# Layer 0 of a four-layer graph network: the key and query products of four blocks by Strassen's seven half-size products

## The chip, the core and the metric

The kernel runs as one program on one core of a Trainium2 chip. The metric is the device time of one execution in microseconds (us), as the median of several runs; lower is better. Everything is computed in fp32.

## What is computed

The network has four layers over a graph of N = 2708 nodes with 512 features each. Each layer adds the result of its graph operation to its input and normalises the rows. The change touches the first step of layer 0, a multi-head attention with 8 heads of 64 dimensions, masked by the adjacency matrix:

```python
keys    = jnp.einsum('nj,hjk->hnk', node_matrix, Wks)
queries = jnp.einsum('nj,hjk->hnk', node_matrix, Wqs)
values  = jnp.einsum('nj,hjk->hnk', node_matrix, Wvs)
atts = jnp.einsum('hqk,hmk->hqm', queries, keys) / key_dim ** 0.5
atts = atts - 1e+16 * (1.0 - adj)[None, :, :]
atts = jax.nn.softmax(atts, axis=-1)
return jnp.einsum('hqm,hmk,hko->qo', atts, values, Wo)
```

Taken over all heads, keys, queries and values are each one product of the 2708x512 node matrix with a 512x512 weight matrix.

## The kernel before

**Projections.** The nodes are split into NB = 6 blocks of 512 columns of the transposed node matrix; the last, block 5, has only 148. A block is loaded into the tile `xb` (128 partitions, KC = 4 slices of the 512 features, up to 512 nodes; two buffers). For each block in turn, 0 to 5, the loop at L215 does three projections. Keys: for each of the NP = 4 groups of 128 output features, `project_in` (L227 to L237) accumulates four matmuls of 128x128 weights with 512 moving columns in one PSUM bank, and the result is copied into `KT` by `evac`, which sends copies to VectorE (L85) and ScalarE (L87) in turn. Block 0 has its four groups interleaved (L243), so that the first slices can be used as they land. Values: GpSimd first makes `xp`, a copy of the block with its columns in another order (L264, one buffer), and for each 128 nodes four matmuls (L269) with 512 moving columns go into `V`. Queries: `project_in` again, with ScalarE scaling by 1/8 on the way out into `qb` (L280, two buffers), and GpSimd's queue stores `qb` to DRAM tiles `qtd`, 128 nodes at a time (L283). The pool `ps_0` gives these products four of the eight PSUM banks.

After block 3 has been written down (L284), the code loads the adjacency rows of the first 128 nodes, sums and masks them, and loads their queries back from `qtd` as `qt` (L177).

After the loop, eight slices of a weight matrix `gw` that layer 2 needs are loaded, multiplied by a vector `ga` and reduced to `u` (L294 to L299). They depend on nothing in layer 0, so that this work runs early, next to block 0.

**Attention.** Then come 84 pairs of a group of 128 query nodes and a pair of heads, and one last item for the remaining 20 nodes. The order on TensorE, VectorE and ScalarE is written out by hand here. `pss` (L329) are the scores, for which VectorE adds the mask and takes maxima (L351, into `s`), ScalarE takes exponentials (L373), VectorE transposes (L380) into `d`, DMAs deal out `d` to `e` (L390), and `av` (L436) sums the values. The scores of the first pair need `qt` of the first chunk and all of `KT`. They use four PSUM banks of the pool `ps_s`; before, these are the four that `ps_0` has not used.

**What sets the order in the projections.** A scheduler orders each engine's instructions by when it expects their inputs. Each engine then works through its own list without overtaking, and waits are semaphores. TensorE's list follows the program: K, V, Q of block 0, of block 1, and so on, then the first scores.

**Layer 3** already uses seven products of halves for a multiplication with the adjacency matrix (L1160), with 512 moving columns, and with 256 in its last group of nodes.

Of the kernel before, what the change touches and what calls it, by code (L numbers as in the profile page):

```python
# [8 lines left out]
F32 = mybir.dt.float32  # L9
AF = mybir.ActivationFunctionType  # L10
ALU = mybir.AluOpType
AX = mybir.AxisListType
PSUM = bass.MemoryType.PSUM
DRAM = bass.MemoryType.DRAM

P = 128
BLK = 512
# [5 lines left out]
def kernel(  # L23
# [22 lines left out]
    nc = tc.nc  # L46
    N, D = x.shape
    KD = 64
    NP = wq.shape[1] // P
    KC = D // P  # L50
    NC = (N + P - 1) // P
    NB = (N + BLK - 1) // BLK
    QSCALE = 1.0 / KD**0.5

    def rows(c):
        return c * P, min(P, N - c * P)

    def cols(b):
        return b * BLK, min(BLK, N - b * BLK)

    def chunks_of(b):
        n0, w = cols(b)
        return [n0 // P + i for i in range((w + P - 1) // P)]
# [18 lines left out]
    def evac(dst, src, every=2):  # L82
        turn[0] += 1
        if turn[0] % every == 0:
            nc.vector.tensor_copy(dst, src)  # L85
        else:
            nc.scalar.copy(dst, src)  # L87
# [24 lines left out]
    def load_rows(t, src):  # L112
        nc.sync.dma_start(t, src.rearrange("(k p) f -> p k f", p=P))
# [24 lines left out]
    with ExitStack() as l0:  # L138
# [3 lines left out]
        KT = kvp.tile([P, NP, N], F32, tag="KT", name="KT")  # L142
        V = kvp.tile([P, NC, D], F32, tag="V", name="V")
# [4 lines left out]
        qtd = [dram.tile([P, NP, rows(c)[1]], F32, tag=f"qtd{c}", name=f"qtd{c}") for c in range(NC)]  # L148
# [58 lines left out]
            nc.scalar.activation(a, a, AF.Identity, scale=1e16, bias=far)  # L207

        with tc.tile_pool(name="kvw", bufs=1) as kvw, tc.tile_pool(name="xTb", bufs=2) as xtp, tc.tile_pool(
            name="ps_0", bufs=4, space=PSUM  # L210
        ) as ps_0:
            wk_sb = kvw.tile([P, KC, D], F32, tag="wk", name="wk_sb")
            wv_sb = kvw.tile([P, KC, D], F32, tag="wv", name="wv_sb")
            wq_sb = kvw.tile([P, KC, D], F32, tag="wq", name="wq_sb")
            for b in range(NB):  # L215
                n0, w = cols(b)
                xb = xtp.tile([P, KC, BLK], F32, tag="xb", name=f"xb{b}")
                if b == 0:
                    for k in range(KC):
                        nc.sync.dma_start(wk_sb[:, k, :], wk[k * P : (k + 1) * P, :])  # L220
                        nc.sync.dma_start(xb[:, k, :w], xT[k * P : (k + 1) * P, n0 : n0 + w])
                    load_rows(wv_sb, wv)
                    load_rows(wq_sb, wq)
                else:
                    load_rows(xb[:, :, :w], xT[:, n0 : n0 + w])

                def project_in(w_sb, p, name):  # L227
                    ps = ps_0.tile([P, BLK], F32, tag="t", name=name)
                    for k in range(KC):
                        nc.tensor.matmul(  # L230
                            ps[:, :w],
                            w_sb[:, k, p * P : (p + 1) * P],
                            xb[:, k, :w],
                            start=(k == 0),
                            stop=(k == KC - 1),
                        )
                    return ps  # L237

                if b == 0:
                    pk = [ps_0.tile([P, BLK], F32, tag="t", name=f"psk0_{p}") for p in range(NP)]  # L240
                    for k in range(KC):
                        for p in range(NP):
                            nc.tensor.matmul(  # L243
                                pk[p][:, :w],
                                wk_sb[:, k, p * P : (p + 1) * P],
                                xb[:, k, :w],
                                start=(k == 0),
                                stop=(k == KC - 1),
                            )
                else:  # L250
                    pk = (project_in(wk_sb, p, f"psk{b}_{p}") for p in range(NP))
                for p, ps in enumerate(pk):
                    evac(KT[:, p, n0 : n0 + w], ps[:, :w])


                xp = xtp.tile([P, KC, BLK], F32, tag="xp", name=f"xp{b}", bufs=1)
                for c in chunks_of(b):
                    o, q = rows(c)[0] - n0, rows(c)[1]
                    src = xb[:, :, o : o + q]
                    dst = xp[:, :, o : o + q]  # L260
                    if c < ND:
                        src = src.rearrange("p k (i x) -> p k x i", i=KD4)
                        dst = dst.rearrange("p k (x i) -> p k x i", i=KD4)
                    nc.gpsimd.tensor_copy(dst, src)  # L264
                for c in chunks_of(b):
                    r0, q = rows(c)
                    ps = ps_0.tile([P, BLK], F32, tag="t", name=f"psv{c}")
                    for k in range(KC):
                        nc.tensor.matmul(  # L269
                            ps[:q, :],  # L270
                            xp[:, k, r0 - n0 : r0 - n0 + q],
                            wv_sb[:, k, :],
                            start=(k == 0),
                            stop=(k == KC - 1),
                        )
                    evac(V[:q, c, :], ps[:q, :])
                qb = xtp.tile([P, NP, BLK], F32, tag="qb", name=f"qb{b}")
                for p in range(NP):
                    ps = project_in(wq_sb, p, f"psq{b}_{p}")
                    nc.scalar.mul(qb[:, p, :w], ps[:, :w], QSCALE)  # L280
                for c in chunks_of(b):
                    r0, q = rows(c)
                    nc.gpsimd.dma_start(qtd[c], qb[:, :, r0 - n0 : r0 - n0 + q])  # L283
                if b == NB - 3:  # L284
                    for k in range(NW + 1):
                        load_chunk(0, k)
                    for k in range(NW):
                        row_sums(0, k)
                        loops(0, k)
                        mask(0, k)  # L290

            ga_sb = kvw.tile([P, D], F32, tag="ga", name="ga_sb")
            pr = kvw.tile([P, D], F32, tag="pr", name="pr")
            nc.sync.dma_start(ga_sb, ga.partition_broadcast(P))  # L294
            for k in range(2 * KC):
                gw_sb = kvw.tile([P, D], F32, tag="gw", name=f"gw{k}", bufs=2)
                nc.sync.dma_start(gw_sb, gw[k * P : (k + 1) * P, :])
                nc.vector.tensor_tensor(pr, gw_sb, ga_sb, ALU.mult)
                nc.vector.tensor_reduce(u[:, k : k + 1], pr, AX.X, ALU.add)  # L299
# [241 lines left out]
        with tc.manual_schedule(  # L541
            engines={mybir.EngineType.PE, mybir.EngineType.DVE, mybir.EngineType.Activation}
        ):
            for i in range(len(items) + 3):
# [4 lines left out]
                if i < len(items):  # L549
                    c, p = items[i]  # L550
# [48 lines left out]
    xtp = ctx.enter_context(tc.tile_pool(name="xtp", bufs=2))  # L599
# [77 lines left out]
    with tc.tile_pool(name="wo", bufs=1, reuse_waits="tile") as wop:  # L677
        wo_sb = wop.tile([P, KC, D], F32, tag="wo", name="wo_sb")
        load_rows(wo_sb, wo)
        for c in range(NC):  # L680
            r0, q = rows(c)
# [6 lines left out]
            for j in range(2):  # L688
                dst = rb[j * KD : (j + 1) * KD]
                dst = dst[:, :, :q] if c == LAST else dst.rearrange("k p q -> k (p q)")  # L690
# [54 lines left out]
    def product(acc, m, values, moving, w, m0=0, m1=NC):  # L745

        mr = rows(m)[1]
        for k in range(KC):
            g = 32 * k if m == NC - 1 else 0
            nc.tensor.matmul(  # L750
                acc[k][:, :w],
                last[0][g : g + mr, :] if m == NC - 1 else values[:mr, k * P : (k + 1) * P],
                moving[g : g + mr, :w],
                start=(m == m0),
                stop=(m == m1 - 1),
            )
# [60 lines left out]
    if True:  # L817
# [19 lines left out]
        for c in range(NC):  # L837
            q = rows(c)[1]
# [94 lines left out]
        for b in range(NB):  # L933
            for m, _ in enumerate(graph1(b)):
# [6 lines left out]
                if b == NB - 2 and m in (3, 7, 11, 15):  # L941
                    c = first[(m - 3) // 4]
                    top0(c, 0, piece(c, 0))
                if b == NB - 1 and m < len(first):
                    c = first[m]
# [79 lines left out]
    if True:  # L1025
# [53 lines left out]
        for b in range(NB):  # L1079
            if b:  # L1080
                queue = Maxima(b + 1) if b + 1 < NB else None
            for m in graph2(b):
                if m % 4 == 2 and 0 <= m // 4 < len(chunks_of(b)) and b:
                    c = chunks_of(b)[m // 4]
                    q = rows(c)[1]
# [24 lines left out]
    with tc.tile_pool(name="zp", bufs=2) as zp:  # L1110
        w3_sb = main.tile([P, KC, D], F32, tag="fcw", name="w3_sb")
        NH = 10
        F = D // 2
        FC = F // P
# [12 lines left out]
        combined = {}  # L1127
# [27 lines left out]
        def banks(name):  # L1155
            return [ps_acc.tile([P, BLK], F32, tag="acc", name=f"{name}_{k}") for k in range(FC)]
# [41 lines left out]
        w = cols(TAIL)[1]  # L1198
        acc = accs("3_t")
        order = [m for i in range(NH) for m in (i, NH + i)] + [NC - 2, NC - 1]  # L1200
# [19 lines left out]
        n0 = 0  # L1220
        while n0 < NH * P:
            w = min(BLK, NH * P - n0)
            n1 = NH * P + n0
            nchunks = w // P
            j = n0 // BLK

            m5, m2, m1 = banks(f"m5_{j}"), banks(f"m2_{j}"), banks(f"m1_{j}")
            for m in range(NH):
                b11, b22 = edges(m, n0, w, f"a{j}"), edges(NH + m, n1, w, f"a{j}")
# [23 lines left out]
            for m in range(NH):  # L1253
                b21, b11, b22 = edges(NH + m, n0, w, f"b{j}"), edges(m, n0, w, f"c{j}"), edges(NH + m, n1, w, f"c{j}")
# [12 lines left out]
            for m in range(NH):  # L1267
                b12, b22, b11 = edges(m, n1, w, f"e{j}"), edges(NH + m, n1, w, f"f{j}"), edges(m, n0, w, f"f{j}")
# [59 lines left out]
```

## Time and profile before

| what | value |
|---|---|
| median of 3 runs | 2588.55 us (2586.21 to 2588.58) |
| the profiled execution | 2589.45 us |
| span of its trace | 2587.7 us |
| TensorE busy | 2532.2 us, 98% of the span |
| VectorE busy | 1874.8 us, 72% |
| ScalarE busy | 1211.7 us, 47% |
| GpSimd busy | 314.0 us, 12% |
| mean granted TensorE clock | 0.991 of full speed |
| TensorE busy from 60 to 227 us | 167.00 of 167.00 us |
| VectorE busy in the same stretch | 11.69 us |
| ScalarE busy in the same stretch | 19.79 us |
| GpSimd busy in the same stretch | 23.08 us |

The times are those of one profiled execution; 1.75 us of it lie outside its span. An engine counts as busy while an instruction is in flight on it. The last four rows are the projections of layer 0 from block 1 on. The trace records each fp32 matmul as two instructions ("records" below), each with its own weight load: the 16 matmuls of a projection of a block appear as x32. A record's own length includes the time to run through the array and overlaps the next one, so the pace of a stream is read from the start times.

### The profile page before, as it was taken

To read this page: it belongs to the slowest core of one execution; us is meant where nothing else is said; L and a number is where in the kernel's file an instruction comes from. 1 tells how busy PE (TensorE), PEld (TensorE's weight loads), DVE (VectorE), ACT (ScalarE), POOL (GpSimd) and SP (SyncE) were. 2 spreads that over 40 slices of the span, in tenths; PEclk is the share of its full clock that TensorE was granted. 3 is DMA by queue.
4 is the path that set the end of the run, shared out by engine and by line. 5 is a ranking of instruction groups with operands and counts; after the bars stand their busy time and mean duration, and the time that the engine had idled before them with its cause. 6 is when DMAs were issued, how large, how long until landed. Compare 5 with 4: busy or idle time off the path is not lost.

```text
span 2587.7 us, 42022 instructions
## 1 busy us (share of the span) xinstructions
PE 2532.2 (98%) x15263; PEld 1468.0 (57%) x15263; DVE 1874.8 (72%) x4576; ACT 1211.7 (47%) x2417; POOL 314.0 (12%) x322
## 2 busy tenths in 40 slices
PE   9999999999999999999899999899999999999997
PEld 4445676766776767676556444444444466444465
DVE  2004999999999999999484777988776874443544
ACT  2113878788787787887111001565665640000000
POOL 2110000000000000000220000343333430000000
PEclk9999999999999999999899999999999999999999
DMA  5112888888888888888763444454433213644633
GB/s 201 33 54 69 217 233 212 232 216 213 234 212 212 233 213 222 225 210 199 215 201 87 125 124 145 119 158 137 124 108 116 64 31 111 186 139 144 178 102 106
DMA packets 221499, 411.42 MB, mean 159 GB/s; under 512 B 28765, under 2 KB 48911, under 8 KB 221292
## 3 DMA queue, kind: packets, MB, share of 16 engines
q1 hardware_dynamic: 215052, 392.00, 55.5%
q0 software_dynamic: 6240, 16.73, 1.7%
q8 instruction: 121, 1.98, 0.3%
q14 instruction: 86, 0.70, 0.1%
HBM read 213.55 MB, written 16.72 MB: 89 GB/s over the span
## 4 chain that ended last, share of the span: by engine, by line
PE 79%; issue 9%; DVE 7%; DMA 2%; ACT 1%; SPq 1%; POOL 0%; POOLq 0%; DVEq 0%; ACTq 0%
PE pss L329 15%; PE av L436 15%; PE acc L750 13%; PE acc L856 7%; PE m L1160 6%; PE pf L762 3%; PE psv L269 3%; PE pst L409 3%; PE psq L230 3%; PE psk L230 2%; PE ph L842 1%; PE acc_0a L750 1%; DVE d L380 1%; DMA e<-d 1%; DVE s L351 1%
## 5 line engine op out<-in xcount | busy, mean ns | idle before, releaser
L351 DVE CUSTOM_DVE_ANT_0 s<-pss,adj 128x512 f32<-128x512 f32 (+1 forms) x1020 | 574.5, 619 | 27.3 <-PE pss L329 25.4
L373 ACT ACTIVATE s<-s,nm 128x1024 f32<-128x1024 f32 (+1 forms) x510 | 527.7, 1037 | 17.3 <-DVE nm L366 15.5
L329 PE MATMUL pss<-KT,qt 64*128 64x512 f32 (+1 forms) x2016 | 459.5, 565 | 4.0 <-DVE mx L351 3.9
L380 DVE STREAM_TRANSPOSE d<-s 128x1024 f32<-128x1024 f32 x340 | 402.4, 1222 | 9.4 <-DMA e<-d 6.5
L750 PE MATMUL acc<-pt,x 128*128 128x512 f32 (+1 forms) x880 | 336.2, 541 | 9.7 <-ACT pt L803 9.7
L436 PEld LDWEIGHTS av<-e,V 128*64 128x64 f32 x5376 | 294.6, 137 | 62.7 <-DMA e<-d 46.2
L436 PE MATMUL av<-e,V 128*64 128x128 f32 x5376 | 326.3, 274 | 0.0
L329 PEld LDWEIGHTS pss<-KT,qt 64*128 64x128 f32 x2016 | 191.1, 186 | 139.9 <-issue 67.2
L750 PEld LDWEIGHTS acc<-pt,x 128*128 128x128 f32 x880 | 159.4, 194 | 186.1 <-issue 162.8
L856 PE MATMUL acc<-at,h 128*128 128x512 f32 (+1 forms) x504 | 196.8, 543 | 0.0
L814 POOL TENSOR_TENSOR cs<-cs,pt 128x512 f32<-128x512 f32 (+2 forms) x110 | 157.6, 1433 | 202.2 <-ACT pt L803 199.8
L801 DVE TENSOR_TENSOR pt<-pt,at 128x512 f32<-128x512 f32 (+2 forms) x132 | 109.0, 833 | 76.4 <-ACT pt L800 76.2
L457 POOL DMA_DIRECT2D otd<-ot x84 | 45.3, 540 | 954.9 <-ACT ot L456 942.5
L1190 ACT ACTIVATE z<-pz,rdeg 128x512 f32<-128x512 f32 (+1 forms) x22 | 15.1, 688 | 311.5 <-PE pz L762 311.5
L93 ACT ACTIVATE ln_t<-lnve 128x1 f32<-128x1 f32 x88 | 17.7, 201 | 305.3 <-DVE lnve L107 305.2
L856 PEld LDWEIGHTS acc<-at,h 128*128 128x128 f32 x504 | 90.2, 190 | 101.4 <-issue 99.0
L410 ACT COPY pt<-pst 128x512 f32<-128x512 f32 x170 | 91.5, 589 | 120.0 <-PE pst L409 119.8
L436 PEld LDWEIGHTS av<-pt,V 128*64 128x64 f32 x1680 | 90.0, 136 | 64.6 <-ACT adj L187 46.2
L803 ACT ACTIVATE pt<-pt 128x512 f32<-128x512 f32 (+2 forms) x132 | 76.1, 579 | 102.8 <-DVE pt L802 102.6
L867 DVE SCALAR_TENSOR_TENSOR cs<-at,rdeg,cs 128x512 f32<-128x512 f32 (+2 forms) x126 | 86.2, 684 | 41.9 <-DMA at<-in_adjT_dram 40.9
L436 PE MATMUL av<-pt,V 128*64 128x128 f32 x1680 | 110.3, 278 | 1.4 <-ACT ot L456 1.4
L85 DVE COPY KT<-psk 128x512 f32<-128x512 f32 (+1 forms) x12 | 7.5, 629 | 131.6 <-PE psk L230 113.9
(299 smaller groups left out, 3563.7 us busy)
## 6 DMA issues: line engine op xcount, KB each, us to landing
e<-d SPq DMA_DIRECT2D x680, 256.0 KB
at<-in_adjT_dram SPq DMA_DIRECT2D x210, 256.0 KB
a<-in_adj_dram SPq DMA_DIRECT2D x38, 677.0 KB
adj<-in_adj_dram SPq DMA_DIRECT2D x42, 512.0 KB
at_a<-in_adjT_dram SPq DMA_DIRECT2D x40, 256.0 KB
at_c<-in_adjT_dram SPq DMA_DIRECT2D x40, 256.0 KB
at_f<-in_adjT_dram SPq DMA_DIRECT2D x40, 256.0 KB
adj<-in_adj_dram SPq DMA_DIRECT2D x21, 330.0 KB
```

Of the source, the lines that this page charges most:

```text
L230: nc.tensor.matmul(ps[:, :w], w_sb[:, k, p * P : (p + 1) * P], xb[:, k, :w], start=(k == 0), stop=(k == KC - 1),)
L329: nc.tensor.matmul(pss[j][:, :w], qt[h, self.p, :], KT[h, self.p, n0 : n0 + w], start=True, stop=True)
L351: nc.vector.tensor_tensor_reduce(out=s[:, j, h0 : h0 + hw], in0=pss[j][:, :hw], in1=a[:, n0 + h0 : n0 + h0 + hw], scale=1.0, scalar=LOW, o ...
L373: nc.scalar.activation(s, s, AF.Exp, bias=self.nm[j], accum_out=self.sums(j, k))
L380: nc.vector.transpose(self.D[k][:, :, j].rearrange("p i m x -> p m i x"), self.s[k][:, j, : n * P].rearrange("p (m i x) -> p m i x", i=KD4 ...
L410: nc.scalar.copy(sb, pt)
L436: nc.tensor.matmul(self.av[j * KD : (j + 1) * KD, out], V[:, m, h * KD : (h + 1) * KD], weights[j], start=(self.done == 0), stop=(self.don ...
L750: nc.tensor.matmul(acc[k][:, :w], last[0][g : g + mr, :] if m == NC - 1 else values[:mr, k * P : (k + 1) * P], moving[g : g + mr, :w], sta ...
L801: nc.vector.tensor_tensor(pt[:mr, :w], pt[:mr, :w], at[:mr, :w], ALU.subtract)
L814: nc.gpsimd.tensor_tensor(sums[:mr, :w], sums[:mr, :w], pt[:mr, :w], ALU.add)
L856: nc.tensor.matmul(acc[hc][:, :w], lastH[g : g + mr, :] if m == NC - 1 else H[m][:mr, hc * P : (hc + 1) * P], at[g : g + mr, :w], start=(m ...
L1160: nc.tensor.matmul(acc[k][:, : moving.shape[1]], combined[which, m][:, k * P : (k + 1) * P], moving, start=(m == 0), stop=(stop and m == N ...
```

## The change

Blocks 1 to 4 get their keys and queries from Strassen's scheme. The 512x512 weights and the 512x512 block are each split into quarters of 256x256. From sums and differences of quarters, seven products of 256x256 with 256x256 are formed, each as two groups of two matmuls with 128x128 weights and 256 moving columns, in one PSUM bank: 28 matmuls of 256 columns for a projection of a block, where 16 of 512 columns stood. The sums of weight quarters (`combined`) are made once for each matrix, two of the five in place, so they come after the short block, whose keys and queries still use the plain weights; the query weights are scaled by 1/8 beforehand. The five sums of quarters of the block (`xs`) are made once for each block and serve both projections. The results of the seven products are put together by two ScalarE copies and eight VectorE additions or subtractions that read PSUM and the destination.

The blocks now come in the order 0, 5, 1, 2, 3, 4, and in each block queries stand in front of values. `ps_0` has all eight PSUM banks, `qb` has one buffer, the values of blocks 1 to 4 are evacuated by ScalarE alone, and the loop over `gw` uses slices of the tile `wk_sb` in place of its own tiles, so that it comes after the last key product.

```diff
-            name="ps_0", bufs=4, space=PSUM
+            name="ps_0", bufs=8, space=PSUM
...
-            for b in range(NB):
+            F = D // 2
+            FC = F // P
+
+            def quarter(t, i, j, n0=0):
+
+                return t[:, i * FC : (i + 1) * FC, n0 + j * F : n0 + (j + 1) * F]
+
+            def combined(w_sb, name):
+
+                a11, a12, a21, a22 = (quarter(w_sb, j, i) for i in range(2) for j in range(2))
+                t = kvw.tile([P, 3, FC, F], F32, tag=f"c{name}", name=f"c{name}")
+                nc.vector.tensor_tensor(t[:, 0], a11, a22, ALU.add)
+                nc.vector.tensor_tensor(t[:, 1], a21, a11, ALU.subtract)
+                nc.vector.tensor_tensor(t[:, 2], a12, a22, ALU.subtract)
+                nc.vector.tensor_tensor(a21, a21, a22, ALU.add)
+                nc.vector.tensor_tensor(a12, a12, a11, ALU.add)
+                return {1: t[:, 0], 2: a21, 3: a11, 4: a22, 5: a12, 6: t[:, 1], 7: t[:, 2]}
+
+            def halves(ws, xs, dst, n0, name):
+
+
+                def product(i):
+                    ps = ps_0.tile([P, FC, F], F32, tag="t", name=f"{name}_{i}")
+                    for p in range(FC):
+                        for k in range(FC):
+                            nc.tensor.matmul(
+                                ps[:, p, :],
+                                ws[i][:, k, p * P : (p + 1) * P],
+                                xs[i][:, k, :],
+                                start=(k == 0),
+                                stop=(k == FC - 1),
+                            )
+                    return ps
+
+                d11, d12, d21, d22 = (quarter(dst, i, j, n0) for i in range(2) for j in range(2))
+                nc.scalar.copy(d12, product(5))
+                nc.scalar.copy(d21, product(2))
+                m1 = product(1)
+                nc.vector.tensor_tensor(d11, m1, d12, ALU.subtract)
+                nc.vector.tensor_tensor(d22, m1, d21, ALU.subtract)
+                for i, ds in ((4, (d11, d21)), (7, (d11,)), (3, (d12, d22)), (6, (d22,))):
+                    m = product(i)
+                    for d in ds:
+                        nc.vector.tensor_tensor(d, d, m, ALU.add)
+
+            order = [0, NB - 1] + list(range(1, NB - 1))
+            for b in order:
                 n0, w = cols(b)
+                whole = b not in order[:2]
...
-                if b == 0:
+                if b == order[2]:
+                    nc.scalar.mul(wq_sb, wq_sb, QSCALE)
+                    wk_c, wq_c = combined(wk_sb, "k"), combined(wq_sb, "q")
+                if whole:
+                    b11, b12, b21, b22 = (quarter(xb, i, j) for i in range(2) for j in range(2))
+                    t = xtp.tile([P, 5, FC, F], F32, tag="xs", name=f"xs{b}", bufs=1)
+                    for i, (x0, x1, op) in enumerate(
...
+                        nc.vector.tensor_tensor(t[:, i], x0, x1, op)
+                    xs = {5: b22, 2: b11, 1: t[:, 0], 4: t[:, 1], 7: t[:, 2], 3: t[:, 3], 6: t[:, 4]}
+                    halves(wk_c, xs, KT, n0, f"psk{b}")
+                    pk = ()
+                elif b == 0:
...
+                qb = xtp.tile([P, NP, BLK], F32, tag="qb", name=f"qb{b}", bufs=1)
+                if whole:
+                    halves(wq_c, xs, qb, 0, f"psq{b}")
+                for p in range(0 if whole else NP):
+                    ps = project_in(wq_sb, p, f"psq{b}_{p}")
+                    nc.scalar.mul(qb[:, p, :w], ps[:, :w], QSCALE)
+                for c in chunks_of(b):
+                    r0, q = rows(c)
+                    nc.gpsimd.dma_start(qtd[c], qb[:, :, r0 - n0 : r0 - n0 + q])
...
-                    evac(V[:q, c, :], ps[:q, :])
-                qb = xtp.tile([P, NP, BLK], F32, tag="qb", name=f"qb{b}")
...
-                if b == NB - 3:
+                    (nc.scalar.copy if whole else evac)(V[:q, c, :], ps[:q, :])
+                if b == order[-3]:
...
-            ga_sb = kvw.tile([P, D], F32, tag="ga", name="ga_sb")
-            pr = kvw.tile([P, D], F32, tag="pr", name="pr")
+            ga_sb = wk_sb[:, 0, :]
+            pr = wk_sb[:, 1, :]
...
-                gw_sb = kvw.tile([P, D], F32, tag="gw", name=f"gw{k}", bufs=2)
+                gw_sb = wk_sb[:, 2 + k % 2, :]
```

More of the change, by code (lines that the diff above doesn't have):

```diff
@@ L237, in project_in @@
                     return ps
-                if b == 0:
+                if b == order[2]:
[5 more added lines that the diff above has]
+                    for i, (x0, x1, op) in enumerate(
+                        (
+                            (b11, b22, ALU.add),
+                            (b21, b11, ALU.subtract),
+                            (b21, b22, ALU.add),
+                            (b12, b22, ALU.subtract),
+                            (b11, b12, ALU.add),
+                        )
+                    ):
+                        nc.vector.tensor_tensor(t[:, i], x0, x1, op)
[3 more added lines that the diff above has]
+                elif b == 0:
                     pk = [ps_0.tile([P, BLK], F32, tag="t", name=f"psk0_{p}") for p in range(NP)]
@@ L275 @@
                         )
-                    evac(V[:q, c, :], ps[:q, :])
-                qb = xtp.tile([P, NP, BLK], F32, tag="qb", name=f"qb{b}")
[L278 to L283, printed above, removed]
-                if b == NB - 3:
+                    (nc.scalar.copy if whole else evac)(V[:q, c, :], ps[:q, :])
+                if b == order[-3]:
                     for k in range(NW + 1):
```

## Prediction

> **What bounds the kernel now.** I read the shares by engine first: TensorE is busy for 98% of the span. An average says little of one stage, so next I read the chain of waits from the start to the first attention pairs, which tells whose time sets the end there. Its columns are start, length (both us) and what held the chain.
>
> ```profile
> 4.16 15.81 PE psk L243 x32
> 19.97 13.73 PE psv L269 x32
> 33.70 13.73 PE psq L230 x32
> 47.44 13.73 PE psk L230 x32
> ...
> 198.50 13.73 PE psq L230 x32
> 212.24 4.03 PE psk L230 x32
> 216.26 6.97 PE psv L269 x16
> 223.24 4.22 PE psq L230 x32
> 227.46 1.92 PE pss L329 x8
> ```
>
> From 4.16 to 227.46 us the chain is TensorE alone, projection after projection without a gap; the granted clock there is 1.00. A microsecond of matmul removed here is one gained, unless a new wait appears. A full projection is 32 records of 0.429 us. In this stretch VectorE is busy for 28.00 us, ScalarE for 32.73, GpSimd for 36.83: wide cover for new side work.
>
> **The products.** Each of eight projections (K and Q, blocks 1 to 4) loses 16 matmuls of 512 columns and gets 28 of 256. Layer 3's last node group runs that very form, fp32, new 128x128 weights for each matmul. The timeline of TensorE there:
>
> ```profile
> 2479.84 1.89 PE L1160 MATMUL m<-at_a,x 128*128 128x256 f32 x8
> 2481.57 1.03 PE L1160 MATMUL m<-ja,wc 128*128 128x256 f32 x4
> 2482.43 1.89 PE L1160 MATMUL m<-at_a,x 128*128 128x256 f32 x8
> ...
> 2490.20 1.89 PE L1160 MATMUL m<-at_a,x 128*128 128x256 f32 x8
> ```
>
> The starts tell the pace: 12 records from 2479.84 to 2482.43, and 48 to 2490.20, 10.36 us, so 0.2158 us each. 28 matmuls are 56 records: 12.09 us in place of 13.73, 1.65 saved, **13.2 us over eight**. The other work (K, Q, V of blocks 0 and 5, V of blocks 1 to 4) keeps its matmuls.
>
> [...] In the trace the ratio is 0.2158/0.429 = 0.503, with weight loads of 190 ns inside the 216. The short block's 148-column matmuls go faster still, 4.03/32 = 0.126 us. I take the row; the projections would break even at 13.73/56 = 0.245 us a record.
>
> **VectorE.** Each block gets 8 additions for K, 8 for Q, and 5 sums for `xs`. Layer 3's gather from PSUM is the same operation, and the `gw` product is the one with two SBUF inputs:
>
> ```profile
> L1250 DVE TENSOR_TENSOR yt_0b<-yt_0b,m 128x512 f32<-128x512 f32 x6 | 3.9, 674 | 0.0
> ```
> ```profile
> 30.86 0.69 DVE L298 TENSOR_TENSOR pr<-gw,ga_sb 128x512 f32<-128x512 f32 x1 [0.54 <-DMA gw<-in_gw_dram]
> ...
> 34.35 1.11 DVE L298 TENSOR_TENSOR pr<-gw,ga_sb 128x512 f32<-128x512 f32 x1
> ```
> ```profile
> 33.83 5.10 POOL L264 COPY xp<-xb 128x512 f32<-128x512 f32 x4 [20.12 <-PE psv L269]
> ```
>
> The columns are groups (count, busy us, mean ns, idle before) in the first, start and length in the others. 16 x 0.67 + 5 x 0.69 = 14.2 us. A product from SBUF takes 1.11 us where GpSimd's `xp` copies run beside it, 0.69 alone. [...] Priced by that for all five sums it is 16.3 us; either is under half of the block's 12.09 + 12.09 + 13.73 = 37.9 us, so both give nothing on the path. With eight banks and seven products, a bank is used again only eight products later, over 10 us, before TensorE would feel a late VectorE. ScalarE: four copies and four V copies, 8 x 0.6 = 4.8 us a block. Hidden.
>
> **The joints**, on my own clock for the new order (block 0 ends at 47.4 as before; block 5 takes 4.03 + 4.22 + 6.97 = 15.2, to 62.7; then four times 37.9, to 214.3):
> - *Q of block 0 in front of V.* It needs `wq_sb` at 19.97 instead of 33.7. When that lands is read from the DMA-issuing queue: an adjacency load waited 2.2 us for `wq_sb` and went out at 14.62, so it was there 5 us early. If it were not, each us late costs one. V then comes later than its data: nothing.
> - *`xp` of block 5* can start only when V of block 0 has read the single buffer (47.4); the queue holds `qtd` stores (36 to 40 us) before it. A copy takes 1.3 to 1.6 us beside others, V of block 5 starts at 55.7: hidden, with 6 us to spare. Later blocks have 24 us for 5.1.
> - *In-place weight sums.* K's wait for block 5's K (51.5) and take 1.4 us; first use at 62.7. The scaling of `wq_sb` is 2048 columns on ScalarE (two of the 1.06 us activations of L187, so about 2.1) after block 5's Q (55.7), the five sums 3.5 to 5.6: done at 61 to 64, first use at 62.7 + 12.1 = 74.8. Behind them on VectorE stands one evacuation of V. Hidden.
> - *`xs`, one buffer.* For the next block it waits for Q's last product; V's 13.7 us cover its 3.5 to 5.6.
> - *`qb`, one buffer.* ScalarE's first Q copy waits for the last block's four stores: 5.6 us to landing and about 0.8 each to issue, some 9 us against the 25.8 of V and K. Hidden; behind it would queue V's copies.
> - *`xb` loads* wait for queries now issued earlier, and land over 20 us ahead. The two `qt` loads stand in front of block 2's on SP; they wait for stores landed by about 44.
> - *The `gw` loop* moves from 21.9-41.6 us, under block 0, to behind K of block 4 (ends 188.5): 9 loads on SP, 8 products, 8 reductions. Before, eight passes took 19.7 us beside adjacency loads. From 189.4 that gives 209.1, under Q and V, which end at 214.3. Its VectorE instructions stand among Q's additions and hold them up, but V's last product needs the oldest of those banks only at 210.9.
> - *First scores.* The new list has a wait on ScalarE in front of the first `pss`, which before waits for its queries alone: with eight banks in `ps_0` the score banks were just used by V. The last V copy starts with V's end and takes 0.59 us (`evac`, L87); with signalling I take **0.75 us**. Bounds: 0 if the wait is for an earlier copy, 1.2 if the chain restarts cold (scores to VectorE took 1.2 before). VectorE paces what follows, so a late first score shifts everything.
>
> From there on nothing is changed. **Sum** against the profiled execution: span 2587.7 - 13.2 + 0.75 = 2575.3, and with the 1.75 outside 2577.0. It was 0.9 above the median of the runs, so **2576.2 us**.
>
> **Rivals.**
> 1. *The joints leak.* Speaking for it: four buffers become single or shared, and all run on VectorE's list. If each of four block changes costs 1.5 us, +6: 2582. If the `gw` passes take 3.5 us instead of 2.46, they end at 217.4, +3: 2579. Against: the slack worked out above, 5 us at the tightest.
> [...]
> 3. *A break-even.* A leak of 7 us or more, e.g. `wq_sb` late by 7 us or VectorE 2 us late in each projection: about 2586. Little speaks for it.
> 4. *That the program does not do it* is excluded: TensorE's list holds 28 narrow matmuls where 16 stood, and nothing else new.
>
> **How the numbers follow.** The forecast 2576.2 has 0.75, rival 1 0.15, rival 3 0.04, rival 2 0.06. The last is kept at 0.06 because a form measured in one stage can meet other traffic in another. The runs of before differ by 2.4 us, and the bounds of the score wait add -0.75 to +0.45; so the forecast's own range is 2573.5 to 2579. Rival 1 carries the upper end: **2572.5 to 2582**. About 0.2%, 5.2 us, is what a measurement can tell from no change. Faster by more, below 2583.4, are the forecast and nearly all of rival 1: 0.90. Within 0.2%: 0.04. Slower: 0.06.
>
> **What would show it.** Right: the new product line has x56 per projection at starts 0.216 us apart; the chain stays on TensorE; the first `pss` starts at 214.3 to 215.5 us; from first score to end the two traces are equally long. Wrong: a gap of TensorE inside blocks 1 to 4 put down to VectorE (`xs`, additions) or to a store; `u` done after V of block 4; a pace above 0.22.

## The result, and the profile after

| | before | changed |
|---|---|---|
| median of 22 runs each | 2586.85 us (2581.12 to 2590.67) | 2580.05 us (2572.33 to 2587.09) |
| profiled execution, and its span | 2589.45, 2587.7 us | 2579.97, 2578.2 us |
| VectorE busy | 1874.8 us | 1922.1 us |

The ratio of the changed kernel to before is 0.9972, with a 95% interval of 0.9966 to 0.9979: 7.2 us faster (5.4 to 8.8). A difference in us is worked out from the ratio here and below; the quotient of the two medians is not exactly that ratio and can differ from it by 1.5 us. The forecast was 12.4 us, so the time is in the range, on its upper side, and 3.9 us above the point.

The chain of waits of the changed kernel, for the stretch shown of before (start, length, what held the chain):

```profile
4.20 16.15 PE psk L311 x32
20.35 13.73 PE psq L279 x32
34.09 13.73 PE psv L346 x32
47.82 4.03 PE psk L279 x32
51.85 4.03 PE psq L279 x32
55.87 6.97 PE psv L346 x16
62.85 12.29 PE psk L242 x56
75.13 12.09 PE psq L242 x56
87.22 13.73 PE psv L346 x32
...
188.85 12.09 PE psq L242 x56
200.94 13.73 PE psv L346 x32
214.67 1.11 PE pss L399 x4
```

Every projection by seven products is there as x56, at 12.09 us; the first, behind the change from 512 to 256 columns, took 12.29. There is no gap: the pieces follow each other to 214.67 us, where before the scores began at 227.46. **12.8 us are saved at this point.** The joints held too: in the waits of this trace no TensorE record behind the first load waits for another engine or a DMA up to 214.6 us. This is the end of VectorE's timeline in the projections (start, length, engine, line, operation):

```profile
205.77 0.69 DVE L368 TENSOR_TENSOR wk_sb<-wk_sb 128x512 f32<-128x512 f32 x1 [0.76 <-DMA wk_sb<-in_gw_dram]
206.49 0.69 DVE L369 TENSOR_REDUCE u<-wk_sb 128x1 f32<-128x512 f32 x1
215.76 0.69 DVE L421 CUSTOM_DVE_ANT_0 s<-pss,adj 128x512 f32<-128x512 f32 x1 [8.58 <-PE pss L399]
```

The moved `gw` loop is done at 207.2 us, and VectorE then sits idle for 8.58 us until the first score. So the projections and all of their joints are accounted for, and they are not where the difference between 12.8 and 7.2 us lies. It must lie behind the first score, where the order of instructions on TensorE, ScalarE and GpSimd is that of before, and so is VectorE's. (One store of the queries, issued behind the first score before, is done earlier now.)

### The profile page after: what moved, and what is told of

The parts are those of the page before. It is cut to its first block, busy times and chain, and to the rows that moved or that the text cites. A ratio compares the mean times of both kernels' runs of the same rounds, so it can differ in the third digit from the quotient of the medians.

```text
span 2578.2 us, 42561 instructions
## 1 busy us (share of the span) xinstructions
PE 2515.9 (98%) x15455; PEld 1501.4 (58%) x15455; DVE 1922.1 (75%) x4654; ACT 1212.3 (47%) x2418; POOL 312.4 (12%) x322
## 4 chain that ended last, share of the span: by engine, by line
PE 78%; issue 9%; DVE 7%; DMA 3%; ACT 1%; SPq 1%; POOL 0%; POOLq 0%; DVEq 0%; ACTq 0%
PE pss L399 15%; PE av L506 15%; PE acc L820 12%; PE acc L926 7%; PE m L1230 6%; PE psv L346 3%; PE pst L479 3%; PE pf L832 2%; PE po L766 2%; PE psk L242 2%; PE psq L242 2%; DMA e<-d 2%; PE ph L912 1%; DVE d L450 1%; DVE s L421 1%
## 5 line engine op out<-in xcount | busy, mean ns | idle before, releaser
L820 PE MATMUL acc<-pt,x 128*128 128x512 f32 (+1 forms) x880 | 333.4, 537 | 12.4 <-ACT pt L873 9.7
L783 ACT ACTIVATE at<-at,big 128x512 f32<-128x512 f32 (+2 forms) x132 | 83.5, 661 | 29.2 <-DMA at<-in_adjT_dram 29.2
```

What stands on the lines that cost most here:

```text
L820: nc.tensor.matmul(acc[k][:, :w], last[0][g : g + mr, :] if m == NC - 1 else values[:mr, k * P : (k + 1) * P], moving[g : g + mr, :w], sta ...
```

## The experiments

All took the kernel before along on the same chip. The time behind the first score was read from each trace at three points: the start of VectorE's first score instruction, the start of the last copy of `av` of the 84 pairs (the time between these two is called the attention below), and the end of the span. The last column but one is the granted clock in the 34 us behind the first score, the last the mean of the whole span.

| kernel | first score | to last `av` copy | from there to the end | sum behind the first score | clock of the first 34 us | mean granted clock |
|---|---|---|---|---|---|---|
| before | 228.66 | 1008.5 | 1350.5 | 2359.0 | 0.95 | 0.991 |
| before_again | 229.17 | 1008.7 | 1349.9 | 2358.7 | 0.95 | 0.991 |
| order_plain | 228.15 | 1008.1 | 1350.4 | 2358.6 | 0.95 | 0.993 |
| cut13 | 215.32 | 1008.4 | 1350.0 | 2358.4 | 0.95 | 0.993 |
| cut27 | 202.37 | 1010.6 | 1348.4 | 2359.0 | 0.90 | 0.990 |
| changed | 215.76 | 1010.7 | 1351.8 | 2362.4 | 0.95 | 0.993 |
| after_again | 215.15 | 1012.4 | 1348.5 | 2360.9 | 0.90 | 0.992 |
| after_b | 214.99 | 1012.8 | 1344.2 | 2357.0 | 0.90 | 0.994 |
| after_c | 215.17 | 1012.7 | 1352.8 | 2365.5 | 0.90 | 0.990 |
| gw_early | 216.30 | 1013.5 | 1346.5 | 2360.0 | 0.90 | 0.991 |
| strassen_v | 234.66 | 1011.5 | 1351.3 | 2362.7 | 0.90 | 0.986 |
| strassen_v2 | 210.18 | 1008.0 | 1346.8 | 2354.8 | 0.95 | 0.994 |

All but the last two columns are in us. `changed` is the first trace of the changed kernel; after_again, after_b and after_c are three more of it.

**The two kernels once more.** Copies without an edit. For the changed kernel:

> The changed kernel once more. In its first trace the first scores start 12.8 us earlier than before, yet the medians differ by only 6.8 us, so some 5 us are given back between the first scores and the end. Theory CHANGE (the change itself lengthens what follows) and theory ABSORB (what follows gives back part of any time removed in front of it): again 6 to 8 us faster than before. Theory CHANCE (the length of what follows scatters from run to run, alike for both kernels): 11 to 13 us faster.

> The changed kernel a third time, for more runs and one more trace. Its first scores stand 12.8 us earlier in both traces so far; 22 runs gave 7.2 us less than before, 5 more gave 10.9. The attention was 2 to 4 us longer in its two traces than in the four of the other kernels. CHANGE: about 9 us faster than before, attention again above 1010 us. CHANCE: 11 to 13 us faster, attention near 1008.5 us.

> The changed kernel a fourth time. Cutting 27.5 us gave 28.0, so nothing is given back in proportion; the lists of all engines from the second attention pair on are the same as before. CHANCE: 10 to 13 us faster than before, and a part of the trace behind the first scores between 2357 and 2362 us, longer where its mean granted clock is lower. CHANGE: 7 to 9 us faster and never below 2360 us in the mean.

Measured: 2576.09 us beside 2586.93 (ratio 0.9958, 0.9944 to 0.9972), 2575.92 beside 2588.06 (0.9959, 0.9944 to 0.9974), and 2578.22 beside 2590.04 (0.9958, 0.9946 to 0.9970): 10.9, 10.6 and 10.9 us faster. For before:

> The kernel before once more, for a second trace of what follows the first scores: in the first one 2587.7 - 227.5 = 2360.2 us. All theories: within 1.5 us of before in the median. CHANCE wants this length and that of the changed kernel (2578.2 - 214.7 = 2363.5) to overlap from run to run; CHANGE wants it to stay near 2360.

Measured: 2588.92 us, ratio 1.0006 (0.9997 to 1.0015). A kernel measured against itself differs by 1.6 us here (2.0 in the medians, a little more than the 1.5 expected).

What follows: the part of the trace behind the first score was 2357.0, 2360.9, 2362.4 and 2365.5 us in four traces of one and the same program. This scatter of 8.5 us is larger than the 5.6 us that were missing, as CHANCE has it. But CHANCE asked for 11 to 13 us in the first two repeats, and they gave a little less (10.8 and 12.1 by the medians); it asked for at most 2362 us behind the first score in after_c, and that trace is the longest. CHANGE asked for at most 9 us in the repeats, and all gave more; but the attention was above 1010 us in all four traces, as CHANGE has it, against 1008.5 and 1008.7 before. So neither theory holds as it was put. The 16 runs of the three repeats have a mean of 2577.7 us, the 49 of before beside them 2588.0: 10.3 us, with a standard error of 0.9.

**The order without the seven products.**

```diff
-                whole = b not in order[:2]
+                whole = False
...
-                if b == order[2]:
-                    nc.scalar.mul(wq_sb, wq_sb, QSCALE)
-                    wk_c, wq_c = combined(wk_sb, "k"), combined(wq_sb, "q")
```

> The changed order alone (block 5 second, queries in front of values, eight PSUM banks, one qb, the gw loop late in wk_sb), all products as before with 512 columns. The first scores should start within 0.3 us of before's 227.46 us. CHANGE: 4 to 6 us slower than before. ABSORB and CHANCE: within 2 us of before.

Measured: 2588.71 us, ratio 1.0006 (0.9997 to 1.0015), the same as before_again in the same sitting. The first score stood at 228.15 us, 0.5 earlier than before. The new order, the single buffers and the late `gw` loop cost nothing that can be measured, and the attention lasted 1008.1 us; CHANGE cannot lie in them alone.

**A cut of the same size without Strassen, and twice of it.** These two kernels leave out one of the four slices of features, in the keys of four blocks (cut13) or in their keys and queries (cut27). In `project_in` of the kernel before:

```diff
-                    for k in range(KC):
+                    ks = KC - 1 if w_sb is wk_sb and 1 <= b <= 4 else KC
+                    for k in range(ks):
...
-                            stop=(k == KC - 1),
+                            stop=(k == ks - 1),
```

For cut27 the condition on `wk_sb` is dropped.

> The kernel before, in which the keys of blocks 1 to 4 take three of their four slices of 128 features (that part of the product is left out): 16 matmuls of 0.858 us fewer, 13.7 us, and nothing else is changed or moved. The first scores should start at 213.7 us. CHANGE and CHANCE: 13 to 14 us faster. ABSORB: 7 to 9 us faster.

> The kernel before, with keys and queries of blocks 1 to 4 taking three of their four slices of features (that part is left out): 32 matmuls of 0.858 us fewer, 27.5 us; first scores at 200.0 us. Half of it alone gave 11.2 to 11.9 us of 13.7. ABSORB (a share of what is removed comes back later): 22 to 24 us faster. CHANGE and CHANCE: 26.5 to 28.5 us faster.

Measured: cut13 2575.78 us beside 2586.93 (0.9954, 0.9940 to 0.9969: 11.9 us, 8.0 to 15.5), cut27 2560.09 beside 2588.06 (0.9887, 0.9871 to 0.9902: 29.2 us, 25.4 to 33.4). The small cut alone could not decide; its interval holds 13.7 as well as 9. The double cut gave all of its 27.5 (28.0 by the medians), outside of what ABSORB expected. ABSORB falls: no fixed share of what TensorE saves in the projections is given back. This kernel has none of the seven products, and yet its attention lasted 1010.6 us.

**The `gw` loop back in its old place.** The loop is moved into block 0, in the space of `xs`:

```diff
+                if b == 0:
+                    g = xtp.tile([P, 5, FC, F], F32, tag="xs", name="gws", bufs=1).rearrange("p a c f -> p a (c f)")
+                    ga_sb = g[:, 0, :]
+                    pr = g[:, 1, :]
...
+                        gw_sb = g[:, 2 + k % 3, :]
...
-            ga_sb = wk_sb[:, 0, :]
-            pr = wk_sb[:, 1, :]
```

> The changed kernel with the gw loop back beside block 0 (its tiles in the space of xs, which is not yet in use there). If the loop's new place behind the last key product is what lengthens the attention: first scores where they were (214.7 us), attention back to 1008.5, 12 to 13 us faster than before. Under CHANCE, and if another part of the change is the cause: as the changed kernel, within 2 us.

Measured: 2578.06 us beside 2588.06 (0.9958, 0.9945 to 0.9970: 10.9 us), attention 1013.5. As the changed kernel. So the late place of the loop is not what lengthens the attention.

**Values by seven products too.** In strassen_v the permuted copy `xp` of blocks 1 to 4 is split as the weights were, with five sums made by VectorE behind the queries (in the space of `xs`), and the quarters of `wv_sb` are combined once:

```diff
+                    tv = kvw.tile([P, 3, FC, F], F32, tag="cv", name="cv")
...
+                    wv_m = {5: v22, 2: v11, 1: tv[:, 0], 4: tv[:, 1], 7: v21, 3: tv[:, 2], 6: v12}
...
+                    t = xtp.tile([P, 5, FC, F], F32, tag="xs", name=f"xv{b}", bufs=1)
+                    halves(combined(xp, "x", t), wv_m, V[:, b * FC * 2 : (b + 1) * FC * 2, :], 0, f"psv{b}", (7, 6, 4, 3))
```

> gw_early with the values of blocks 1 to 4 by seven products too: four more projections at 12.09 us in place of 13.73, 6.6 us less on TensorE, first scores near 208.1 us. VectorE gets 8 additions and 5 sums more per block, about 9 us of 36. CHANCE: 6 to 7 us below gw_early and 18 to 19.5 below before. ABSORB: about 4 to 5 below gw_early. If VectorE's sums for the values come too late behind the last query addition, TensorE waits up to 1 us in each block and the gain over gw_early falls to 2.5.

Measured: 2597.83 us, ratio 1.0037 (1.0024 to 1.0050): 9.6 us *slower* than before, though TensorE has 6.6 us less to do than in gw_early. The chain of waits shows why (start, length, what held it):

```profile
74.80 12.10 PE psq L243 x56
86.90 0.02 issue
86.92 0.69 DVE qb L263
87.61 0.60 DVE xv L229
88.21 0.60 DVE xv L230
88.82 0.60 DVE xv L231
89.42 0.60 DVE xp L232
90.02 0.61 DVE xp L233
90.63 0.14 issue
90.77 15.24 PE psv L243 x56
```

The first two products of the scheme (5 and 2) use the two sums that are made in place. These overwrite quarters that the other three sums read, so they come last, and TensorE stands through the last query addition and all five sums: 3.87 us. That was the failure the expectation named, but put at 1 us. And the wait is only a part of the loss. The table of stretches (busy time of TensorE, its weight loads, VectorE, ScalarE, GpSimd, then the granted clock, the DMA share and GB/s) has the rest:

```profile
62.52:86.90 24.38, 24.37 (x112) 21.12 (x112) 11.96 (x17) 2.34 (x4) 6.52 (x6) 1.00 0.17 60
86.90:90.77 3.87, 0.00 (x1) 0.04 (x1) 3.69 (x6) 0.00 (x0) 1.45 (x2) 0.88 0.42 170
90.77:106.01 15.24, 15.24 (x57) 12.96 (x58) 5.39 (x9) 1.17 (x2) 0.00 (x0) 0.81 0.00 1
...
134.06:148.07 14.01, 14.01 (x57) 12.06 (x58) 5.38 (x9) 1.17 (x2) 0.00 (x0) 0.88 0.01 1
```

After each wait the same 56 records take 14.0 to 15.2 us instead of 12.1, behind the first two at a granted clock of 0.81 and 0.88. One wait of 3.9 us so costs 5.8 to 7.0. Over four blocks 15.5 us of waits and 10.1 of slower records come to 25.6, against 6.6 saved, 19.0 us more. In gw_early V ended at 215.2 us, with block 0 and 5 done 0.9 us later than here; so V should end at 233.3, and it ended at 233.46.

**The same with the products in another order.** strassen_v2 begins each block's values with the two products whose block side is a plain quarter (3 and 4), so that the sums run beside them:

```diff
+                for i, ds in ((3, (d12, d22)), (4, (d21, d11))):
+                    m = product(i)
+                    for d in ds:
+                        nc.scalar.copy(d, m)
+                add, sub = ALU.add, ALU.subtract
+                for i, ds in (
+                    (1, ((d11, add), (d22, add))),
+                    (7, ((d11, add),)),
+                    (6, ((d22, add),)),
+                    (2, ((d21, add), (d22, sub))),
+                    (5, ((d12, add), (d11, sub))),
+                ):
```

> strassen_v with the products of the values in another order: the two that use plain quarters of the block (3 and 4) first, so that VectorE's sums run beside them instead of in front of them. In strassen_v TensorE waited 3.9 us in each of four blocks, and a stretch of half clock followed each wait. If the late sums are the whole cause of its loss, the waits and the half-clock stretches inside the projections go, the first scores start at 208 to 209.5 us, 6 us before gw_early, and the time is 5 to 7 us below gw_early, 16 to 18 below before. If the fault lies in VectorE's total load, waits of over 1 us per block remain, and the time is no better than the changed kernel's.

Measured: 2567.76 us beside 2590.04 (0.9919, 0.9903 to 0.9936): 21.0 us faster than before (16.6 to 25.1), more than the 16 to 18 expected. Its chain in the projections is TensorE again, without a wait:

```profile
63.71 12.29 PE psk L243 x56
75.99 12.09 PE psq L243 x56
88.08 12.09 PE psv L279 x56
...
196.86 12.10 PE psv L279 x56
208.96 0.02 issue
208.98 1.29 DVE V L303 x2
210.27 0.60 DVE s L476
```

The granted clock from 63.71 to 208.96 us is 1.00. At the end the last two additions for V stand in front of the first score on VectorE, but they cost next to nothing: from V's end to that score it is 1.2 us, where the changed kernel takes 1.1. This version beats both kernels; after_c, in the same sitting, took 2578.22 us.

## Why the prediction was right, and where its size was off

- *Pace of the narrow products.* Right: 12.09 us a projection, from layer 3's row. A record of 256 columns took 0.216 us, 0.503 of the 0.429 at 512 columns, and less than the 0.245 at which nothing would be saved. At full clock no run shows a dearer narrow product, on which the chance of 0.06 for a slower kernel rested.
- *VectorE hidden.* Right. The sums for `xs` ran in 3.09 us behind Q, under V; no record of TensorE in the projections waits for VectorE.
- *The joints.* Right one by one: `wq_sb` in front, weight sums, `xs`, `qb`, `xb`. The `gw` loop ended at 207.2 us where 209.1 was forecast. The tightest slack in the forecast's own list was not 5 us but 1.8 (209.1 against 210.9, when V needs the banks); the last query addition was done at 203.0. order_plain, which has the order, the banks, the single `qb` and the late loop but no sums, shows these at no measurable cost.
- *First scores.* The forecast charged 0.75 us for a wait on ScalarE. It cost nothing: from V's end to VectorE's first score 1.09 us (214.67 to 215.76), before 1.20. The lower bound, 0, was right: TensorE's scores start at once, so the wait was for an earlier copy. In its place 0.4 us were lost in the first key product, 16.15 us in this trace and 15.81 in before's, which is unchanged code. The chain reached the scores 12.8 us earlier; the sum had 13.2 less the 0.75.
- *"From there on nothing is changed."* This is the step that failed, in size. The lists of instructions are indeed the same, but the time they take is not a constant to be carried over, and the sign that both traces would be equally long from the first score on did not come: the time was 2357.0 to 2365.5 us in four traces of one program, and before's 2359.0 was used as if it were exact. The own range of the forecast, 2573.5 to 2579, came from the spread of three runs, 2.4 us; 22 runs of the changed kernel spread over 14.8. That the time of the first 22 runs landed inside the stated range is luck: the upper end is owed to rival 1, whose mechanism, a leak at the joints, did not happen. The repeats, 2575.9 to 2578.2, lie in the forecast's own range.
- *What stays open.* The projections give 12.8 us in the first pair of traces, and 13.6 between the mean first scores of all traces of the two kernels (228.9 and 215.3). The first 22 runs gave 7.2 and the repeats 10.3, with a standard error of 0.9. Proportional giving back, the order, and the place of the `gw` loop are excluded by cut27, order_plain and gw_early. All four sittings of the changed kernel, and gw_early, gave less than the projections did, so chance alone hardly makes up the rest. In the traces the rest lies in the attention, which took 1012.2 us in the mean of four traces and 1008.6 in the two of before, 3.6 us more; from there to the end both took 1349 to 1350. The seven products by themselves do not explain it: cut27 has none of them and took 1010.6 us, strassen_v2 has more and took 1008.0. What goes with a long attention is the clock at its start: 0.90 in six traces of 1010.6 to 1013.5 us, 0.95 in five of 1008.0 to 1008.7 and in the first trace of the changed kernel, the one exception with 1010.7. The mean clock of whole runs does not differ, 0.9917 in the 16 repeats and in the 49 runs of before beside them. Why the changed kernel met the slower start in three of four traces, whether that makes the whole rest, and why the first sitting lay lower still, these runs don't settle.

## What to carry to other kernels

Where one engine was busy without a gap and another had time, Strassen's scheme on halves paid here in fp32 at 256 columns, with 12.09 us a projection in place of 13.73. Take the pace of the narrow matmul from the start times of a stream in the same trace (records of 256 columns were 0.379 us long here, and 0.216 us apart). Begin each group with the products that need no sums, because behind the waits of some 4 us on TensorE the slower records cost two thirds as much again here (10.1 us behind 15.5). And when a saving is under half a per cent, split the trace at the point to which the change reaches: up to there it can be forecast to a few tenths of a us, behind it only to the scatter of the rest.

## What the runs showed of the hardware

*The waits of strassen_v were paid twice.* Gaps of 3.9 us on TensorE were each followed by 56 records that took 1.9 to 3.1 us longer than 12.09, behind the first two at a mean clock of 0.81 and 0.88. For these two waits, the 3.41 us ahead of the fall of the granted clock, and the stretch at half clock (columns as in the table of stretches):

```profile
86.44:89.85 3.41, 0.45 (x3) 0.04 (x1) 2.97 (x6) 0.00 (x0) 1.45 (x2) 1.00 0.38 154
89.85:96.68 6.83, 5.91 (x14) 4.78 (x15) 0.77 (x2) 0.58 (x1) 0.00 (x0) 0.50 0.09 38
...
130.81:134.22 3.41, 0.16 (x1) 0.19 (x2) 3.11 (x6) 0.00 (x0) 1.45 (x2) 1.00 0.38 154
134.22:137.63 3.41, 3.41 (x9) 2.70 (x9) 0.00 (x0) 0.00 (x0) 0.00 (x0) 0.50 0.02 5
```

Behind 3.41 us in which TensorE worked 0.45 or 0.16 us, the clock was halved. It stayed so for 6.83 us where the wait reached into the slow stretch, to 90.77, and for 3.41 where TensorE worked throughout. Half of the work in these stretches, 2.96 and 1.71 us, differs by as much as 15.24 and 14.01 us do; the records behind the third and fourth wait took 15.23 and 14.03 us. TensorE was idle throughout in neither of the two stretches ahead of a fall. Behind the first scores of before even 3.41 us with 2.31 us of work (239.97 to 243.38) were followed by 3.41 us at 0.50; in strassen_v 3.41 us with 2.78 us of work (127.40 to 130.81) were not. How much idle time it takes to lower the clock, these runs don't show.

*Time and clock go together from run to run.* Between the first score and the first copy of `av` TensorE waits 2.2 us for VectorE in the first trace of the changed kernel, and the chain of waits there runs through the deal of `d` (4.78 us). Two traces of the changed program there (columns as above):

```profile
215.76:249.40 33.64, 31.36 (x190) 18.14 (x188) 32.67 (x96) 22.41 (x43) 0.00 (x0) 0.95 0.49 113
```
```profile
215.17:250.11 34.94, 32.71 (x190) 18.81 (x188) 32.66 (x96) 22.40 (x42) 0.00 (x0) 0.90 0.47 108
```

The first is the first trace, the second after_c: the same instructions, 1.3 us apart, at clocks of 0.95 and 0.90. The table of the experiments has this clock for every trace. Over the 22 runs of the changed kernel time and mean clock go together with a correlation of -0.74, about 2 us for each thousandth of clock. So much of the scatter goes with the clock; that the clock makes it, and not a wait that slows both, is not shown.
